# First attention of a two-layer graph-attention block: tiles 0 and 1 of a group as one task, tiles 2 and 3 one by one

## The chip, the core and the metric

The kernel runs on one core of one Trainium2 chip. The metric is the time of one execution in device microseconds (us). The kernel before has 6 runs, between 2294.36 and 2296.16 us, with a median of 2295.54 us. One execution was profiled.

## The reference

The input x has 128 batches of 64 nodes with 512 features. One 64 x 64 adjacency matrix holds for all batches. Everything is float32.

```python
def gat(x, adj, W, a):                      # [B,N,F] -> [B,H,N,O], all heads
    Wh = einsum('bnf,hfo->bhno', x, W)
    f1, f2 = Wh @ a[:, :O], Wh @ a[:, O:]
    e = f1[:, :, :, None] + f2[:, :, None, :]
    e = where(e > 0, e, 0.01 * e)
    e = where(adj > 0, e, -1e9)
    return einsum('bhnm,bhmo->bhno', softmax(e), Wh)

h = relu(layernorm(x))                      # 128 x 64 x 512
h = elu(gat(h, adj, W_heads, a_heads))      # 4 heads of 512, put side by side
out = elu(gat(h, adj, W_out, a_out))        # one head of 512
y = relu(out @ w1 + b1) @ w2 + b2 + out
return x + layernorm(y) * gamma + beta
```

## The kernel before

**Tiles and groups.** The 8192 rows (128 batches of 64) are 64 tiles of 128 rows: two batches in a tile. Four tiles make a group, and there are 16 groups (G = 4, NG = 16, lines 64 and 65). The large products (the first projection, the second projection, the two products of the feed-forward part) are done per group by a Winograd-like scheme with seven sub-products in place of eight (`unit`, line 242); a sub-product is a run of matmuls of 128 x 128 weights on 256 columns.

**First attention before the first projection.** From group 1 on, the attention weights of the first layer are applied to the normalized rows *before* the projection: per tile, `attend1` (lines 526 to 563) multiplies HN (the normalized rows, 128 x 512, line 345) with AT (the transposed attention weights, line 488) and writes the blocks z11, z12, zS1 and z22, which the first projection (`project1`, line 588) reads one group later. A tile holds two batches, rows 0 to 63 and rows 64 to 127, and each batch has its own matmul: the matmuls at line 547 contract over 64 rows, with b = 0 on the upper half of TensorE's rows and b = 1 on the lower half, and each b has a PSUM bank of its own. A tile has two halves of its features ("11" and "12" for tiles 0 and 1, "S1" and "22" for tiles 2 and 3). In the code a half is four matmuls; in the profile each float32 matmul has two records, so a half is 8 records and a tile 16. Half 0 writes two auxiliary PSUM banks (`aux`, line 93: 2 banks), half 1 writes two banks of the ring (`bank`, line 80: 6 banks). Each bank is then copied to z: b = 0 by ScalarE (line 559), b = 1 by VectorE (line 561). All other matmuls around this place use all 128 rows of TensorE.

**Where the tasks stand.** The main loop (line 948) goes over the groups. For a group g from 1 on it runs `project1(g)`, the first projection, whose last head's end stands just ahead of what concerns us: the ELU of its results (lines 571 to 573, on ScalarE and VectorE) still reads ring banks. Then comes `project2(g)` (line 677), 28 steps, each four matmuls in the code and eight records in the profile. Beside these steps `run` (line 233) spreads other work evenly: `first`, a list of 14 entries (lines 972 to 975), stands first in it, and holds the four attention tasks of the next group, the four transposes of the group before (`transpose_out`, line 777: four 128 x 128 transposes on TensorE, a copy on ScalarE at line 783, an addition on GpSimd at line 784), the normalization of two pairs of tiles of the group after next, and entries that do nothing. Their order in the groups 1 to 13 is: attention 0, transpose 0, nothing, attention 1, transpose 1, norms, nothing, attention 2, transpose 2, nothing, norms, attention 3, transpose 3, nothing. In group 14 there are no norms. Group 0 takes its attention tasks out of a table written by hand (lines 977 to 997).

**What sets the order.** Each engine executes its instructions in the order in which the program was built, and waits at semaphores. The weights of each sub-product come by DMA on the SyncE queue (SP in the profile) into a ring of 11 buffers (`piece`, line 211, tile w); a load waits until TensorE is done with the buffer that it takes. On GpSimd (POOL), `project2` also subtracts blocks of H1 head by head as TensorE finishes with each (line 688). The banks of the ring are given out in turn among those that are free first; each task thus waits for the last reader of the bank that it gets.

Of the kernel before, what the change touches and what calls it, by code (L numbers as in the profile page):

```python
# [9 lines left out]
FP = mybir.dt.float32  # L10
# [12 lines left out]
def gat_preln_kernel(  # L23
# [30 lines left out]
    nc = tc.nc  # L54
    P = 128
    B, N, F = x.shape
    H = W_heads.shape[0]
# [3 lines left out]
    NB = P // N  # L61
    KC = F // P
    NT = B * N // P
    G = 4
    NG = NT // G
    Q = O // 2
    T = 2 * P
# [6 lines left out]
    big = ctx.enter_context(tc.tile_pool(name="big", bufs=1))  # L74
# [5 lines left out]
    def bank(name):  # L80
        return ps.tile([P, 2, T], FP, tag="mm", name=name)
# [11 lines left out]
    def aux(shape, name):  # L93
        return ps.tile(shape, FP, tag="aux", name=name, bufs=2)
# [7 lines left out]
    X, HN, HNS, AT = {}, {}, {}, {}  # L102
# [126 lines left out]
    def flush_late():  # L229
        while late:  # L230
            late.pop(0)()

    def run(steps, side=()):

        side, done = list(side), 0
        for i, fn in enumerate(steps):
            fn()
            while done * len(steps) < (i + 1) * len(side):
                side[done]()
                done += 1  # L240
# [229 lines left out]
    def attn_weights(p):  # L470
        A1[p] = softmax(E1.pop(p), None, 2 * H, "s1", p)
# [23 lines left out]
    def stage_a(g):  # L495


        if g >= NG:
            return [], [], []
        p, r = 2 * g, 2 * g + 1  # L500

        def norms(p):
            norm1(2 * p)
            norm1(2 * p + 1)
            if p >= 2:
                ahead = 2 * p + (4 if p < 4 else 2)
                prefetch(ahead)
                prefetch(ahead + 1)

        def transposes(p):  # L510
            transpose_h(2 * p)
            transpose_h(2 * p + 1)

        return (
            [lambda: norms(p), lambda: norms(r)],
            [
                lambda: transposes(p), lambda: transposes(r), nothing, lambda: project_f(g), nothing,
                lambda: (scores1(g), attn_weights(p)), nothing, lambda: attn_weights(r),
            ],
            [nothing, lambda: transpose_weights(p), nothing, nothing, lambda: transpose_weights(r)],  # L520
        )
# [1 line left out]

    ZB = {}

    def attend1(g):
        z = {}
        ZB[g] = z

        def task(j):  # L530

            t = G * g + j
            at = AT[t]
            done = []
            for half in range(2):
                nm = ("11", "12")[half] if j < 2 else ("S1", "22")[half]
                if nm not in z:
                    z[nm] = big.tile([P, H, 2, T], FP, tag="z" + nm, name=f"z{nm}_{g}")
                src, off = (HNS[t], 0) if nm == "S1" else (HN[t], half * T)
                if half == 1:  # L540
                    banks = [bank(f"pz{nm}_{t}_{b}") for b in range(NB)]
                else:
                    banks = [aux([P, 2, T], f"pz{nm}_{t}_{b}") for b in range(NB)]
                for c in range(2):
                    for b in range(NB):
                        rows = slice(b * N, (b + 1) * N)
                        nc.tensor.matmul(
                            banks[b][:, c, :].rearrange("p (h n) -> p h n", h=H),
                            src[rows, off + c * P:off + (c + 1) * P],
                            at[rows, b], start=True, stop=True, skip_group_check=True,  # L550
                        )
                done.append((nm, banks))
            for nm, banks in done:
                for b in range(NB):
                    n0 = (j % 2) * P + b * N
                    dst = z[nm][:, :, :, n0:n0 + N].rearrange("p h c n -> p c h n")
                    srcv = banks[b].rearrange("p c (h n) -> p c h n", h=H)
                    if b == 0:
                        nc.scalar.copy(dst, srcv)
                    else:  # L560
                        nc.vector.tensor_copy(dst, srcv)

        return [lambda j=j: task(j) for j in range(G)]


    H1, ZSUM = {}, {}
# [11 lines left out]
    def z_sums(g, h):  # L578
        z = ZB[g]
        ZSUM[h] = new_sums(f"z{g}_{h}")  # L580
        sums(nc.gpsimd, z["S1"][:, h], z["11"][:, h], z["12"][:, h], z["22"][:, h], *ZSUM[h])
# [124 lines left out]
    def scores2(g, j):  # L706
        if j == 0:
            F2[g] = sm.tile([P, 2, G], FP, tag="f2", name=f"f2_{g}")
        f = F2[g]
        for c in range(2):  # L710
            junk = wk.tile([P, FO], FP, tag="elu", name=f"jf{g}_{j}_{c}", bufs=3)
            nc.vector.scalar_tensor_tensor(  # L712
                junk, WH2[g][:, j], 1.0, ao[:, c, :], ALU.mult, ALU.mult,
                accum_out=f[:, c, j:j + 1],
            )
# [45 lines left out]
    def stage_e(g):  # L761

        gap = [lambda: None]
        score = [lambda j=j: scores2(g, j) for j in range(G)]
        attend = [lambda q=q: attend2(g, q) for q in range(2)]
        return (
            gap + score + [lambda: spread2(g)] + gap * 2 + [lambda: softmax2(g)] + gap * 5
            + [lambda: transpose_weights2(g)] + gap * 2 + attend[0:1] + gap * 2 + attend[1:2] + gap * 4
        )
# [79 lines left out]
    def mix(*lists):  # L849

        lists = [l for l in lists if l]
        keyed = [((i + 0.5) / len(l), n, fn) for n, l in enumerate(lists) for i, fn in enumerate(l)]
        return [fn for _, _, fn in sorted(keyed, key=lambda k: k[:2])]
# [16 lines left out]
    norms, scores, turns = stage_a(1)  # L870
# [77 lines left out]
    for g in range(NG):  # L948
        if g >= 1:
            side = stage_e(g - 1)  # L950
            done, n = 0, 6 * H
            for i in range(n):
                if i % 6 == 0:
                    steps = project1(g, i // 6)
                steps[i % 6]()
                while done * n < (i + 1) * len(side):
                    side[done]()
                    done += 1
            flush_late()
        attn = attend1(g + 1) if g + 1 < NG else []  # L960
        norms, scores, turns = stage_a(g + 2)
        tr, ff, fin = feed_forward(g - 1) if g >= 1 else ([], [], [])
        if g == NG - 1:
            run(project2(g), tr + [nothing] * 6 + ff[:2])
            run(ff[2:], [
                lambda: [scores2(g, j) for j in range(G)], lambda: spread2(g), nothing, nothing,
                lambda: softmax2(g), *[nothing] * 7, lambda: transpose_weights2(g), nothing,
                *[lambda q=q: attend2(g, q) for q in range(2)], nothing,
            ])
            continue  # L970
        early = [lambda: z_sums(g + 1, 0)] if g else []
        first = mix(attn, tr, [nothing] * len(attn))
        if g >= 1:
            first[5:5] = norms[:1]
            first[10:10] = norms[1:]
        if g == 0:
            side = {
                0: lambda: (attend0(2, 1), turn0(1, 1), project_f(1)),
                1: lambda: (attend0(3, 1), turn0(2, 1)),
                2: lambda: (turn0(3, 1), scores1(1), attn_weights(2), attn_weights(3)),  # L980
                5: lambda: weight_sums(M1, LAST["pe"]),
                7: turns1[1],
                8: lambda: fetch(M2, LAST["pe"]),
                9: attn[0],
                10: lambda: (attn[1](), norms[0](), turns1[4]()),
                12: attn[2],
                13: lambda: (attn[3](), norms[1]()),
                15: scores[0],
                16: scores[1],
                17: lambda: weight_sums(M2, LAST["pe"]),  # L990
                18: scores[3],
                20: scores[5],
                21: scores[7],
                22: lambda: z_sums(g + 1, 0),
                26: turns[1],
                27: lambda: (turns[4](), load_rows()),
            }
            for i, fn in enumerate(project2(g)):
                fn()
                side.get(i, nothing)()  # L1000
        else:
            run(project2(g), first + mix(
                ff[:7] + early + ff[7:12] + fin[:1] + ff[12:13] + fin[1:2] + ff[13:],
                scores + [nothing] * 8,
            ) + mix(fin[2:], [nothing] + turns + [nothing] * 2))
    last = fin
    tr, ff, fin = feed_forward(NG - 1)
# [30 lines left out]
```

## Time and profile before

| | |
|---|---|
| median of 6 runs | 2295.54 us |
| the profiled execution, its own time | 2296.16 us |
| its span, first to last instruction | 2294.2 us |
| around the span (2296.16 - 2294.2) | 1.96 us |
| TensorE matmuls (PE) busy | 2274.1 us |
| TensorE weight loads (PEld) busy | 1890.6 us |
| VectorE (DVE), ScalarE (ACT), GpSimd (POOL) busy | 1274.0, 905.2, 1018.3 us |
| from one group's first attention task to the next group's | 140.37 us |

Busy time of PE counts each matmul from its start to its modelled end, and these overlap; so a busy PE may still lose time between matmuls. What counts is when one matmul starts after another. In the answers of the trace a row of the timeline is a run of like instructions: start in us from the span's start, duration of the run in us, engine, line, operation, what it writes and reads, the shape, and how many; in brackets stands the idle time of the engine ahead of it and what ended it.

### The profile page before, as it was taken

What the parts mean: (1) busy time and instruction counts of PE and PEld (TensorE: products, weight loads), DVE (VectorE), ACT (ScalarE), POOL (GpSimd) and SP (SyncE); (2) the same over time, 40 slices, a digit from 0 to 9 for tenths busy, and PEclk for the clock granted to TensorE, in tenths of its full rate; (3) what the DMA queues carried; (4) which work ended last, traced back from release to release, by engine and by line L of the source; (5) the groups of instructions that cost most, each with busy time, mean ns of one, the idle gap of its engine ahead of it and who ended that gap; (6) DMA issues with size and microseconds to landing.
All of it is one profiled execution on the core that took longest, in us unless ns stands there. A gap on an engine that the chain in (4) does not pass through costs nothing. (4 is left out here: it accounts for less than half of the span.)

```text
span 2294.2 us, 33256 instructions
## 1 busy us (share of the span) xinstructions
PE 2274.1 (99%) x11856; PEld 1890.6 (82%) x11856; DVE 1274.0 (56%) x2227; ACT 905.2 (39%) x1633; POOL 1018.3 (44%) x906
## 2 busy tenths in 40 slices
PE   9999999999999999999999999999999999999997
PEld 4688888888888888888888888888888888888885
DVE  7554654655556555564655646555475554744427
ACT  3535244252542525335253352534425244251512
POOL 7653524444254442634425344352444525533324
PEclk9999999999999999999999999999999999999999
DMA  8553453534535444353544545345354454635543
GB/s 289 194 183 130 147 179 133 180 132 147 175 132 185 136 156 160 135 184 131 166 150 140 182 133 179 130 147 179 133 180 133 147 174 132 183 118 171 160 147 106
DMA packets 255012, 361.15 MB, mean 157 GB/s; under 512 B 23768, under 2 KB 143608, under 8 KB 254848
## 3 DMA queue, kind: packets, MB, share of 16 engines
q1 hardware_dynamic: 250096, 341.93, 46.0%
q0 software_dynamic: 4576, 16.81, 2.0%
q8 instruction: 96, 1.57, 0.3%
q14 instruction: 68, 0.56, 0.1%
q10 hardware_dynamic: 176, 0.28, 0.0%
HBM read 331.66 MB, written 27.26 MB: 156 GB/s over the span
## 5 line engine op out<-in xcount | busy, mean ns | idle before, releaser
L305 PE MATMUL g_b<-w,h 128*128 128x256 f32 x2560 | 593.1, 379 | 0.0
L305 PEld LDWEIGHTS g_b<-w,h 128*128 128x128 f32 x2560 | 481.1, 190 | 64.6 <-issue 2.0
L289 PE MATMUL g_a<-z,w 128*128 128x256 f32 x1440 | 341.7, 380 | 0.0
L289 PE MATMUL g_a<-zs_z,w 128*128 128x256 f32 x1440 | 336.0, 381 | 0.0
L289 PEld LDWEIGHTS g_a<-zs_z,w 128*128 128x128 f32 x1440 | 269.9, 190 | 59.2 <-issue 24.3
L289 PEld LDWEIGHTS g_a<-z,w 128*128 128x128 f32 x1440 | 272.3, 190 | 41.3 <-DVE g_a L603 5.0
L305 PE MATMUL g_b<-w,hS 128*128 128x256 f32 x1024 | 238.2, 379 | 0.0
L607 POOL TENSOR_TENSOR hS<-hS,h 128x512 f32<-128x512 f32 x60 | 78.1, 1302 | 359.9 <-DVE hS L573 359.9
L305 PEld LDWEIGHTS g_b<-w,hS 128*128 128x128 f32 x1024 | 192.1, 190 | 25.0 <-issue 0.2
L571 ACT ACTIVATE exc<-g_a 128x512 f32<-128x512 f32 x240 | 142.6, 594 | 164.1 <-DVE g_a L603 96.2
L573 DVE SCALAR_TENSOR_TENSOR h<-exc,g_a 128x512 f32<-128x512 f32 x180 | 123.4, 686 | 140.9 <-ACT exc L572 140.3
L572 ACT ACTIVATE exc<-exc 128x512 f32<-128x512 f32 x240 | 151.4, 631 | 6.7
L688 POOL TENSOR_TENSOR h<-h,h 128x512 f32<-128x512 f32 x64 | 86.9, 1367 | 138.5 <-PE g_b L305 138.5
L688 POOL TENSOR_TENSOR h<-hS,h 128x512 f32<-128x512 f32 x64 | 81.7, 1277 | 146.2 <-PE g_b L305 146.0
L314 POOL TENSOR_TENSOR zs_z<-zS,z 128x512 f32<-128x512 f32 x60 | 85.3, 1422 | 137.2 <-PE g_a L289 134.0
L489 ACT COPY at<-s1pt 128x512 f32<-128x512 f32 x64 | 34.4, 590 | 268.9 <-PE s1pt L485 268.9
L833 POOL TENSOR_TENSOR xr<-xr,bs 128x512 f32<-128x512 f32 x64 | 96.4, 1510 | 74.3 <-DMA xr<-in_x_dram 44.4
L305 PE MATMUL g_d<-w,rt 128*128 128x256 f32 x512 | 121.8, 380 | 2.3 <-DVE o L825 1.0
L289 PE MATMUL g_c<-ot,w 128*128 128x256 f32 x512 | 122.7, 383 | 0.6 <-DVE ot L792 0.6
L289 PE MATMUL g_a<-zS,w 128*128 128x256 f32 x480 | 113.4, 379 | 0.0
L712 DVE SCALAR_TENSOR_TENSOR jf<-wh,ao 128x512 f32<-128x512 f32 x128 | 98.1, 802 | 26.6 <-ACT wh L694 26.4
L305 PEld LDWEIGHTS g_d<-w,rt 128*128 128x128 f32 x512 | 96.9, 190 | 17.4 <-DVE o L825 2.2
(164 smaller groups left out, 3531.0 us busy)
## 6 DMA issues: line engine op xcount, KB each, us to landing
w<-tc SPq DMA_DIRECT2D x624, 256.0 KB, 2.6
w<-in_L_gnn_W_out_dram SPq DMA_DIRECT2D x192, 256.0 KB, 2.7
w<-in_L_gnn_W_heads_dram SPq DMA_DIRECT2D x180, 256.0 KB, 2.9
w<-in_L_gnn_w_dram SPq DMA_DIRECT2D x96, 256.0 KB, 2.7
x<-in_x_dram SPq DMA_DIRECT2D x64, 256.0 KB, 4.6
xr<-in_x_dram SPq DMA_DIRECT2D x128, 128.0 KB, 2.6
out_dram<-o SPq DMA_DIRECT2D x126, 128.0 KB, 2.4
tc<-pt POOLq DMA_DIRECT2D x20, 512.0 KB, 4.3
```

Of the source, the lines that this page charges most:

```text
L289: LAST["pe"] = nc.tensor.matmul(bk[:, o, :], w[:, k, ts(o, P)], a[:, k, :], start=start and o == 0 and k == 0, stop=k == 1, skip_group_che ...
L305: LAST["pe"] = nc.tensor.matmul(bk[:, j, :], a[:, k, ts(j, P)], w[:, k, :], start=start and n == 0, stop=i == len(ms) - 1 and k == 1, skip ...
L314: eng.tensor_tensor(s2, s1, a11, ALU.subtract)
L489: nc.scalar.copy(AT[t].rearrange("p b h n -> p (b h) n"), pt)
L571: nc.scalar.activation(ex, src, AF.Relu, scale=-1.0)
L572: nc.scalar.activation(ex, ex, AF.Exp, scale=-1.0)
L573: nc.vector.scalar_tensor_tensor(dst, ex, -1.0, src, ALU.add, ALU.max)
L607: nc.gpsimd.tensor_tensor(dst, dst, H1["22"][:, h], ALU.add)
L688: nc.gpsimd.tensor_tensor(dst[:, h], x0[:, h], x1[:, h], ALU.subtract)
L712: nc.vector.scalar_tensor_tensor(junk, WH2[g][:, j], 1.0, ao[:, c, :], ALU.mult, ALU.mult, accum_out=f[:, c, j:j + 1],)
L833: nc.gpsimd.tensor_tensor(xr, xr, bs, ALU.add)
```

## The change

`attend1` gets a second argument, `paired`. Where it is true (in the loop's groups 1 to 14), tiles 0 and 1 are one task of four halves: tile 0 half 0 in the two auxiliary banks, tile 0 half 1 and tile 1 half 0 in two ring banks each, tile 1 half 1 in the two auxiliary banks again. Tiles 2 and 3 stay tasks of their own with the banks as before. The two copies of a half are now written directly behind its matmuls. The list `first` is written out so that the pair stands where attention 0 stood, and an entry that does nothing where attention 1 stood. In group 0 every tile stays a task of its own.

```diff
-    def attend1(g):
+    def attend1(g, paired):
         z = {}
         ZB[g] = z
-        def task(j):
+        def products(j, half, own):
             t = G * g + j
             at = AT[t]
-            done = []
-            for half in range(2):
-                nm = ("11", "12")[half] if j < 2 else ("S1", "22")[half]
...
-                if half == 1:
-                    banks = [bank(f"pz{nm}_{t}_{b}") for b in range(NB)]
+            nm = ("11", "12")[half] if j < 2 else ("S1", "22")[half]
...
+            if own:
+                banks = [aux([P, 2, T], f"pz{nm}_{t}_{b}") for b in range(NB)]
+            else:
+                banks = [bank(f"pz{nm}_{t}_{b}") for b in range(NB)]
+            for c in range(2):
+                for b in range(NB):
+                    rows = slice(b * N, (b + 1) * N)
+                    nc.tensor.matmul(
+                        banks[b][:, c, :].rearrange("p (h n) -> p h n", h=H),
+                        src[rows, off + c * P:off + (c + 1) * P],
+                        at[rows, b], start=True, stop=True, skip_group_check=True,
+                    )
+            for b in range(NB):
+                n0 = (j % 2) * P + b * N
+                dst = z[nm][:, :, :, n0:n0 + N].rearrange("p h c n -> p c h n")
+                srcv = banks[b].rearrange("p c (h n) -> p c h n", h=H)
+                if b == 0:
+                    nc.scalar.copy(dst, srcv)
                 else:
-                    banks = [aux([P, 2, T], f"pz{nm}_{t}_{b}") for b in range(NB)]
...
-        return [lambda j=j: task(j) for j in range(G)]
+                    nc.vector.tensor_copy(dst, srcv)
+        def task(js):
+            steps = [(j, half) for j in js for half in range(2)]
+            for i, (j, half) in enumerate(steps):
+                products(j, half, i == 0 or len(steps) == 4 and i == 3)
+        tiles = [(0, 1), (2,), (3,)] if paired else [(j,) for j in range(G)]
+        return [lambda js=js: task(js) for js in tiles]
...
-        attn = attend1(g + 1) if g + 1 < NG else []
+        attn = attend1(g + 1, g > 0) if g + 1 < NG else []
...
-        first = mix(attn, tr, [nothing] * len(attn))
+        gap = [nothing]
         if g >= 1:
-            first[5:5] = norms[:1]
-            first[10:10] = norms[1:]
+            first = attn[:1] + tr[:1] + gap * 2 + tr[1:2] + norms[:1] + gap
+            first += attn[1:2] + tr[2:3] + gap + norms[1:] + attn[2:] + tr[3:] + gap
```

## The prediction

> **What bounds the kernel.** I read the page first: span, busy time, granted clock. Then the waits of PE, the records of line 547, and last the timeline of PE, ACT and DVE around the four tasks of one group.
>
> ```profile
> span 2294.2 us, 33256 instructions
> PE 2274.1 (99%) x11856; PEld 1890.6 (82%) x11856; DVE 1274.0 (56%) x2227; ACT 905.2 (39%) x1633; POOL 1018.3 (44%) x906
> PEclk9999999999999999999999999999999999999999
> ```
>
> TensorE is busy 99% of the span, in every slice but the last, at full clock (0.998). The page's chain reaches back to 2263 us only, so it says nothing of the middle. The waits of PE say more: the longest in the whole trace are these, at the kernel's start and end.
>
> ```profile
> PE pab L177 <- DMA ar<-in_L_gnn_a_heads_dram: 4.8, 1, 4.8
> PE g_c L289 <- ACT t_c L255: 1.1, 1, 1.1
> ```
>
> So in the middle PE waits for nobody, and only work of TensorE, or time lost between its matmuls, can be saved. Line 547's own view shows such a loss: 58 of its 60 runs of weight loads begin after an idle time of PEld ended by "issue", that is by no other engine.
>
> ```profile
> L547 PE MATMUL pz<-at,hn x720: 376/376/480, 114.2 to 2059.5; 64*128 64x256 f32 x180
>   issue: 19.2, 58
> ```
>
> The PE timeline of the group that starts at 355.35 us tells the price:
>
> ```profile
> 355.35 2.00 PE L547 MATMUL pz<-at,hn 64*128 64x256 f32 x16
> 357.28 0.66 PE L782 MATMUL pto<-ident,o 128*128 128x128 f32 x4
> 357.77 1.89 PE L305 MATMUL g_b<-w,h 128*128 128x256 f32 x8
> 359.60 2.00 PE L547 MATMUL pz<-at,hn 64*128 64x256 f32 x16
> 361.53 0.66 PE L782 MATMUL pto<-ident,o 128*128 128x128 f32 x4
> 362.02 3.62 PE L305 MATMUL g_b<-w,h 128*128 128x256 f32 x16
> ...
> 373.96 1.89 PE L305 MATMUL g_b<-w,hS 128*128 128x256 f32 x8
> 375.69 0.59 PE L289 MATMUL g_c<-ot,w 128*128 128x256 f32 x2
> ```
>
> The last two rows give the undisturbed pace: 8 matmuls of 256 columns take 375.69 - 373.96 = 1.73 us from start to start, 0.216 each. The task at 359.60 is the second one (attention 1), which the change moves.
>
> **What one visit to the 64-row matmuls costs beyond its work.** (1) Before it: 8 full-row matmuls from 357.77 to 359.60 take 1.83 us, not 1.73: 0.10 lost. (2) The task: 16 records in 8 pairs, a pair side by side on the two halves of the rows. At 0.216 a pair this would be 1.73; from 359.60 to 361.53 it is 1.93: 0.20 lost. (3) Behind it, four transposes take 362.02 - 361.53 = 0.49. Without a visit ahead of them they take 0.44:
>
> ```profile
> 2178.15 0.60 PE L782 MATMUL pto<-ident,o 128*128 128x128 f32 x4
> 2178.59 1.89 PE L305 MATMUL g_b<-w,h 128*128 128x256 f32 x8
> ```
>
> so 0.05 is lost. The starts of the single records give the same without rounding: the first 64-row matmul comes 309 ns after the last full-row one (216 undisturbed: 93); the second pair 320 after the first (104); the first transpose 314 after the last pair (98); the second transpose 165 after the first (109 undisturbed: 56). The sum is 351 ns a visit, the same in every group within 3 ns.
>
> **The change, part by part.**
>
> *Removed.* One visit in each of the groups 1 to 14: the matmuls of attention 1 now follow those of attention 0, in the same row mode. That saves 14 x 0.351 = 4.91 us. The built order of the changed kernel agrees: on TensorE the 16 records stand ahead of transpose 0 in just these 14 groups, on ScalarE the copy of transpose 0 stands behind the two added copies, and on VectorE, GpSimd and SyncE the order is the same instruction by instruction. Group 0 has the same order on all engines.
>
> *Moved: transpose 1.* It now stands between full-row matmuls. The rows at 2178.15 show that such a transpose costs nothing beyond 0.44 us, work that it has today too. Cost 0.
>
> *Longer run.* No run in the trace is over 8 pairs. From pair 2 on, pairs come at 0.216 us like every 256-column matmul, in tiles of both kinds. I take 0 for pairs 9 to 16. Bounds: below 0.216 nothing goes, as 0.216 is the pace of all such matmuls here; at worst the start-up of 0.104 is paid once more in the middle, 14 x 0.104 = 1.46 us.
>
> *Added waits: banks.* Let S be the task's start (355.35). Halves 1 to 4 start at S, S + 0.97, S + 1.83 and S + 2.70 (4 pairs of 0.216 a half, and 0.104 once).
>
> ```profile
> 354.15 0.69 DVE L573 SCALAR_TENSOR_TENSOR h<-exc,g_a 128x512 f32<-128x512 f32 x1 [0.46 <-ACT exc L572]
> 355.89 0.69 DVE L573 SCALAR_TENSOR_TENSOR hS<-exc,g_a 128x512 f32<-128x512 f32 x1 [1.05 <-ACT exc L572]
> 356.63 0.69 DVE L561 COPY z<-pz 128x512 f32<-128x512 f32 x1
> ...
> 356.57 0.59 ACT L559 COPY z<-pz 128x512 f32<-128x512 f32 x1 [0.72 <-PE pz L547]
> ```
>
> Half 3 takes the ring banks of the last head's g5 and g1; their last reader is the L573 at 354.15, done at 354.84 = S - 0.51, and their first weight load stands at S + 1.62: 2.1 us to spare. Half 4 takes the auxiliary banks back. Half 1's copies end at 357.16 (ACT) and 357.32 (DVE) = S + 1.97; half 4's first weight load is due a slot ahead of its matmul, at S + 2.48: 0.5 us to spare, in each of the 14 groups (one group has ACT 0.28 us later, still in time). Transpose 0 takes the g6 bank, read until 356.58 and needed at S + 3.4. So I take 0 for the waits. Should the cover of half 4 go, each microsecond that the DVE copy is late beyond those 0.5 costs PE 1 us in each of 14 groups, with everything queued behind it on PE.
>
> *Copies.* Counts are unchanged: eight a pair. A half takes PE 0.864 us and its copies 0.59 on ACT and 0.69 on DVE side by side, so they keep up. ACT's copy of transpose 0 moves from 357.98 to about 359.8, transpose 1's keeps its place; both are read by g_c at 375.69. The additions of L784 on POOL follow.
>
> *Step delayed.* The second step of project2 (8 matmuls at 357.77) comes 1.73 us later. Its weight buffer is released that much later on SP's queue; the load into it is for a piece 11 further on, about 11 x 1.73 = 19 us away, and lands in 2.6 us. The subtraction at L688 that waits for this step (POOL, 359.81) moves to about 361.5, and is read in the p = 6 product after 380. All hidden; with the next step PE is 0.35 us ahead of before, as is every queue that waits for PE.
>
> What is late next? Nothing in the groups: PE has no other wait there, so the gain goes into the end unchanged.
>
> **Two rules of the Trainium skill.** PEld's idle time of 0.33 us ahead of each visit is the row. "TensorEngine Tiling (Array Packing)", Key Properties, says that a change of tiling mode drains TensorE, which agrees; "TensorE: Matmul & The Clock Gate", step-by-step, puts the drain at about 128 cycles, else hidden under the next matmul. By an estimate from that page (128 / 2.4 GHz = 53 ns, twice a visit) the gain would be 14 x 0.107 = 1.5 us, which no one could measure; the trace's 351 ns speak for 4.9. The first page's PSUM Bottleneck section speaks against the change: tiling speeds the matmuls, not the emptying of PSUM; here 0.69 against 0.864 us leaves that rule no hold.
>
> **The sum.** The profiled execution took 2296.16 us, 1.96 of it around the span: 2296.16 - 4.9 = 2291.3 with a span of 2289.3. The profiled run stands 0.62 above the median of the six, so for the median: 2295.54 - 4.9 = 2290.6 us, -0.21%. About 0.2%, 4.6 us, is what a measurement of this kernel can tell from no change, so the forecast lies close to that bound.
>
> **Rivals.**
> 1. *Start-up paid again* inside the 16 pairs, at the change of tile or at half 4's semaphore. For: no such run is in the trace. Against: at today's change of half pairs keep 0.216. Gain 4.91 - 1.46 = 3.45: 2292.1.
> 2. *Given back elsewhere*: some wait on PE, now hidden, takes the 0.35 us a group. For: SP's queue is in order and its loads do wait. Against: no wait on PE, and 19 us of lead. 2295.5. That the visits are not saved, though the order is as said, has the same price.
> 3. *Slower: auxiliary banks late.* Half 4 stalls on the DVE copy of half 1, which stands behind the ELU at L573. It decides when that copy ends after S + 2.48 + 0.35 = S + 2.83 (0.86 later than now). With two more DVE operations of 0.69 ahead of it: S + 3.35, 0.87 - 0.35 = 0.52 lost in 14 groups, 7.3 us: 2302.8. Against: DVE's order is unchanged.
>
> **How the numbers follow.** Forecast 0.84, rival 1 0.08, rival 2 0.05, rival 3 0.03. The six runs lie from 1.18 below to 0.62 above their median, so the forecast's median may miss the 0.2% bound, only 0.3 us away: I count 0.70 of its 0.84 beyond the bound and 0.14 within. Faster 0.70, same 0.14 + 0.08 + 0.05 = 0.27, slower 0.03. The range goes from 2290.6 - 1.2 = 2289.4 to rival 1 with a little scatter, 2292.3.
>
> **What would show it.** In line 547's view of after: 46 visits in place of 60, about 14.6 us of "issue" in place of 19.2 (14 x 0.33 less); one run of 32 records in about 3.73 us (2.00 + 8 x 0.216) ahead of transpose 0; tile 2's task 9.86 us behind S in place of 10.21; 140.02 us from group to group in place of 140.37; still no wait on PE. Wrong if the run of 32 takes over 3.8 us (rival 1 or 3, told apart by whether pair 13 waits for DVE), if the 140.02 fails while the run is right (rival 2), or if the transpose behind the delayed step starts late.

## The result, and the profile after

The changed kernel takes 2289.86 us (median of 19 runs, 2289.07 to 2291.24), the kernel before 2295.07 (39 runs beside them). The ratio is 0.9978, with a 95% interval from 0.9972 to 0.9984: 3.7 to 6.4 us faster. The forecast of 4.9 us lies inside, 2290.6 lies 0.7 above the median, and the range 2289.4 to 2292.3 holds it.

The page of after, its first lines:

```profile
span 2287.7 us, 33256 instructions
PE 2269.1 (99%) x11856; PEld 1892.9 (83%) x11856; DVE 1273.3 (56%) x2227; ACT 905.8 (40%) x1633; POOL 1016.2 (44%) x906
```

As many instructions as before, PE busy for 99% of the span as before. Neither line tells why the span is shorter. The view of the first attention's line (545 now, 547 before) does:

```profile
L545 PE MATMUL pz<-at,hn x720: 376/376/480, 112.9 to 2053.4; 64*128 64x256 f32 x180
...
  issue: 14.6, 44
```

The idle time of PEld ahead of these matmuls that no other engine ends fell from 19.2 us in 58 places to 14.6 in 44: the 14 visits that were forecast, at 0.33 us. The timeline of PE in the group shown before (it now begins at 353.74):

```profile
353.74 3.72 PE L545 MATMUL pz<-at,hn 64*128 64x256 f32 x32
357.39 0.66 PE L785 MATMUL pto<-ident,o 128*128 128x128 f32 x4
357.88 1.89 PE L305 MATMUL g_b<-w,h 128*128 128x256 f32 x8
359.61 0.60 PE L785 MATMUL pto<-ident,o 128*128 128x128 f32 x4
360.05 3.62 PE L305 MATMUL g_b<-w,h 128*128 128x256 f32 x16
363.60 1.14 PE L545 MATMUL pzS<-at,hns 64*128 64x256 f32 x8
```

The run of 32 records lasts 3.72 us (forecast 3.73). Transpose 1, between full-row matmuls, takes 360.05 - 359.61 = 0.44 us, and the 8 matmuls ahead of it 359.61 - 357.88 = 1.73: no loss on either side. Tile 2 follows at 363.60 - 353.74 = 9.86 us, as forecast. From one group's first attention matmul to the next group's, the records give 140.016 us in place of 140.367, twelve times within 3 ns: 0.351 a group.

The cover of half 4 held. In the timeline of the same group the copies of half 1 end at 355.55 (ACT) and 355.70 (DVE); half 4's weight load is due at 353.74 + 2.48 = 356.22:

```profile
354.27 0.69 DVE L576 SCALAR_TENSOR_TENSOR hS<-exc,g_a 128x512 f32<-128x512 f32 x1 [1.05 <-ACT exc L575]
354.96 0.59 ACT L555 COPY z<-pz 128x512 f32<-128x512 f32 x1 [0.72 <-PE pz L545]
355.01 0.69 DVE L557 COPY z<-pz 128x512 f32<-128x512 f32 x1
```

The two profiled executions differ by more, 6.5 us of span. Of these 1.4 lie ahead of the first matmul, which waits for its first DMA (4.8 us before, 3.4 after), and that time varies from run to run (3.8 to 4.3 us in the profiles of the runs below); 4.9 are the 14 groups; 0.2 are left.

### The profile page after: what moved, and what is told of

Its sections match the earlier page's. It is cut to its first block, busy times and chain, and to the rows that moved or that the text cites. A ratio compares the mean times of both kernels' runs of the same rounds, so it can differ in the third digit from the quotient of the medians.

```text
span 2287.7 us, 33256 instructions
## 1 busy us (share of the span) xinstructions
PE 2269.1 (99%) x11856; PEld 1892.9 (83%) x11856; DVE 1273.3 (56%) x2227; ACT 905.8 (40%) x1633; POOL 1016.2 (44%) x906
## 5 line engine op out<-in xcount | busy, mean ns | idle before, releaser
L691 POOL TENSOR_TENSOR h<-h,h 128x512 f32<-128x512 f32 x64 | 86.9, 1366 | 138.5 <-PE g_b L305 138.5
L314 POOL TENSOR_TENSOR zs_z<-zS,z 128x512 f32<-128x512 f32 x60 | 84.8, 1414 | 138.5 <-PE g_a L289 135.2
L691 POOL TENSOR_TENSOR h<-hS,h 128x512 f32<-128x512 f32 x64 | 81.7, 1277 | 138.9 <-PE g_b L305 138.7
L836 POOL TENSOR_TENSOR xr<-xr,bs 128x512 f32<-128x512 f32 x64 | 95.9, 1504 | 74.5 <-DMA xr<-in_x_dram 42.3
L715 DVE SCALAR_TENSOR_TENSOR jf<-wh,ao 128x512 f32<-128x512 f32 x128 | 94.7, 776 | 27.9 <-ACT wh L697 27.7
```

The costliest lines, as they stand in the source:

```text
L314: eng.tensor_tensor(s2, s1, a11, ALU.subtract)
L691: nc.gpsimd.tensor_tensor(dst[:, h], x0[:, h], x1[:, h], ALU.subtract)
L715: nc.vector.scalar_tensor_tensor(junk, WH2[g][:, j], 1.0, ao[:, c, :], ALU.mult, ALU.mult, accum_out=f[:, c, j:j + 1],)
L836: nc.gpsimd.tensor_tensor(xr, xr, bs, ALU.add)
```

## The experiments

All edits are to the changed kernel. "A group" is the distance between the first attention matmuls of two groups, in the profile, the twelve from group 1 to 13; visits are runs of line 545. Ratios are to the kernel before, timed beside each run. The changed kernel has 19 runs, e1, e2, e3 and e3b have 11 each, e4, e5, e6 and e8 five, e9 two.

| kernel | visits | a group, us | median, us | ratio, 95% interval |
|---|---|---|---|---|
| before | 60 | 140.367 | 2295.07 | 1 |
| changed | 46 | 140.016 | 2289.86 | 0.9978, 0.9972 to 0.9984 |
| e1, pair with the old banks | 46 | 140.303 | 2294.99 | 1.0001, 0.9992 to 1.0010 |
| e2, new banks, old places | 60 | 140.367 | 2295.99 | 1.0004, 0.9995 to 1.0013 |
| e3, two pairs | 32 | 140.566 | 2296.98 | 1.0008, 0.9999 to 1.0016 |
| e3b, two pairs, norms later | 32 | 139.713 | 2290.01 | 0.9975, 0.9966 to 0.9984 |
| e4, one visit | 18 | 139.437 | 2281.09 | 0.9940, 0.9927 to 0.9952 |
| e5, one visit, t3 early | 18 | 139.755 | 2286.66 | 0.9963, 0.9950 to 0.9977 |
| e8, one visit, norms early | 18 | 139.314 | 2280.66 | 0.9937, 0.9923 to 0.9950 |
| e6, halves apart | 88 | 141.506 | 2311.26 | 1.0068, 1.0056 to 1.0081 |
| e9, full rows | 46 | 145.870 | 2376.5 | 1.0352, 1.0322 to 1.0382 |

**Theory:** TensorE sets the time; each visit to the 64-row matmuls costs it 0.351 us beyond the work, and the ring banks only keep a longer visit from waiting. **Rivals:** the banks or the copies bring the gain; or the price belongs to something else in the task, such as its operands.

### The price: is it the row mode?

```diff
-                        src[rows, off + c * P:off + (c + 1) * P],
-                        at[rows, b], start=True, ...
+                        src[:, off + c * P:off + (c + 1) * P],
+                        at[:, b], start=True, ...
```

> The changed kernel with its first attention contracted over all 128 rows (the two batches of a tile are added up, so z is another quantity and the outputs are not the reference's; all other work is as it was). Copies, banks, places and waits stay. Each tile's 16 records now run one by one at 0.216 us in place of 8 pairs: 4 x 8 x 0.216 = 6.91 us a group more. Theory (the price of a visit is the change to 64-row matmuls and back): the three visits' 3 x 0.351 = 1.05 us go, 140.02 + 6.91 - 1.05 = 145.87 us a group, and no idle PEld ahead of line 545. Rival (the price comes from the new operands, banks or semaphores of the task): 146.92 us a group, with the idle times still there.

Measured: 145.870 us a group. Line 545 has no idle weight loads left. The timeline of PE:

```profile
364.74 7.07 PE L545 MATMUL pz<-at,hn 128*128 128x256 f32 x32
371.64 0.60 PE L785 MATMUL pto<-ident,o 128*128 128x128 f32 x4
```

32 records take 6.90 us to the transposes, 0.216 each, with nothing lost at either end: the first record of a visit comes 216 ns after the one before it (309 in the changed kernel), and the second transpose 109 ns after the first (165). Same tiles, banks, copies and semaphores: the 0.351 us belong to the change of row mode and back. (What e9 computes is another quantity; only its times are read.)

### The price: does it go by the visit?

e6 takes the pair apart into four visits, with the same banks:

```diff
+        if paired:
+            halves = [lambda i=i: products(i // 2, i % 2, i in (0, 3)) for i in range(4)]
+            return halves + [lambda: task((2,)), lambda: task((3,))]
...
+            first = attn[:1] + tr[:1] + attn[1:2] + gap + attn[2:3] + tr[1:2] + norms[:1] + attn[3:4] + gap
+            first += attn[4:5] + tr[2:3] + gap + norms[1:] + attn[5:] + tr[3:] + gap
```

> The four halves of tiles 0 and 1 as four visits, with work of project2 or a transpose between them, in the changed kernel's banks: 88 visits in place of 46. Theory (each visit has its price, whatever it holds): three more a group, each 0.093 + 0.104 + 0.098 + 0.104 = 0.40 us, as the new ones end in 256-column matmuls; 42 x 0.40 = 16.8 us above the changed kernel's 2289.9: 2306.7, 141.2 us a group. Rival (the price goes with the matmuls in the visit, or hides): under 2300.

Measured: 141.506 us a group, 2311.3 in all; above the forecast, and far from the rival. The timeline of PE around half 3:

```profile
361.00 1.13 PE L545 MATMUL pz<-at,hn 64*128 64x256 f32 x8
362.06 1.99 PE L305 MATMUL g_b<-w,h 128*128 128x256 f32 x8
363.89 0.60 PE L788 MATMUL pto<-ident,o 128*128 128x128 f32 x4
...
369.44 0.92 PE L545 MATMUL pzS<-at,hns 64*128 64x256 f32 x6 [0.23 <-ACT z L555]
```

A half is 4 pairs, 0.864 us; it takes 1.06: 0.20 lost. The 8 matmuls behind it take 1.83 in place of 1.73: 0.10. With 0.10 at the entry that makes the expected 0.40 a visit, 1.20 a group. The other 0.29 are a wait that the expectation missed: tile 2's first matmul waits for ACT's copy of half 4, since half 4, with the auxiliary banks, now stands just ahead of it, and that copy stands behind an hn on ACT. The matmul comes 608 ns after the one before it in place of 309; PE's own idle time shows 0.2 us of this (13 times, 2.9 us in all).

### The banks: e1 and e2

e1 keeps the pair and takes the banks in the old turn; e2 keeps the banks and puts the tiles back:

```diff
 e1
-                products(j, half, i == 0 or len(steps) == 4 and i == 3)
+                products(j, half, half == 0)
 e2
+                products(j, half, half == (paired and j == 1))
-        tiles = [(0, 1), (2,), (3,)] if paired else [(j,) for j in range(G)]
+        tiles = [(j,) for j in range(G)]
...
+            first = attn[:1] + tr[:1] + gap + attn[1:2] + tr[1:2] + norms[:1] + gap
+            first += attn[2:3] + tr[2:3] + gap + norms[1:] + attn[3:] + tr[3:] + gap
```

> Tiles 0 and 1 stand side by side in one task as in the changed kernel, but the banks alternate as before: half 3 (tile 1, half 0) takes the two auxiliary banks again. Theory (a saved visit is worth 0.351 us, and the four ring banks are what keeps PE from waiting): half 3's first weight load is due at S + 1.62 us, and half 1's copies end at S + 1.81 (ACT) and S + 1.97 (DVE); PE stalls 0.3 to 0.6 us in each of 14 groups, so the gain of 0.351 is eaten: 2294.4 to 2298.6 us against 2295.1 before, and a wait on PE or PEld for DVE z or ACT z appears 14 times. Rival (only the place of the task counts, banks are free anyway): 2290, as the changed kernel.

> Four tasks at their old places, so 60 visits as before; but tile 1 takes ring banks for its half 0 and auxiliary banks for its half 1, and the copies are written behind each half, as in the changed kernel. TensorE's order is that of the kernel before. Theory (only the saved visits count): no change, 2295.1 within 0.6 us, 140.37 us from group to group. Rival (the banks or the place of the copies bring the gain): 2290.

e1 measured 2295.0, the gain gone. Its timeline shows the wait:

```profile
354.34 4.01 PE L545 MATMUL pz<-at,hn 64*128 64x256 f32 x32
...
355.56 0.59 ACT L555 COPY z<-pz 128x512 f32<-128x512 f32 x1 [0.72 <-PE pz L545]
...
356.19 1.75 PEld L545 LDWEIGHTS pz<-at,hn 64*128 64x128 f32 x16 [0.26 <-ACT z L555]
```

The run lasts 4.01 us in place of 3.72. Half 3's weight load was due at 354.34 + 1.62 = 355.96 and begins at 356.19, just behind ACT's copy (355.56 + 0.59 = 356.15). That takes 0.29 of the 0.351 us, 14 times; of the 0.06 that are left, 0.9 us in all, its profile loses most again in one place of group 13 (told at the end). So the ring banks are what makes the pair pay; they are needed only because the pair is there. e2 shows the other half of this: with the new banks and copies at the old places a group takes 140.367, exactly as before. Its median is 1.0 us above that of the kernel before beside it, inside its interval but outside the 0.6 us of the expectation; in its profile the same place in group 13, where g_c waits for the sum at L795, loses 0.9 us more than in the kernel before.

### More tiles in a visit: e3, e3b, e4

```diff
 e3
+        tiles = [(0, 1), (2, 3)] if paired else [(j,) for j in range(G)]
+            first = attn[:1] + tr[:1] + gap * 2 + tr[1:2] + norms[:1] + gap
+            first += attn[1:2] + tr[2:3] + gap + norms[1:] + gap + tr[3:] + gap
 e3b: the tiles of e3
+            first = attn[:1] + tr[:1] + gap * 2 + tr[1:2] + gap * 2
+            first += attn[1:2] + norms[:1] + tr[2:3] + norms[1:] + gap + tr[3:] + gap
 e4
+                products(j, half, i % 3 == 0)
+        tiles = [(0, 1, 2, 3)] if paired else [(j,) for j in range(G)]
+            first = attn[:1] + tr[:1] + gap * 2 + tr[1:2] + norms[:1] + gap
+            first += gap + tr[2:3] + gap + norms[1:] + gap + tr[3:] + gap
```

> Tiles 2 and 3 become a second task of four halves at tile 2's place. Two visits a group, so by the saved visits alone 14 x 0.351 = 4.9 us below the changed kernel: 2285.0. But there ScalarE normalizes two tiles (hn, L346) and copies s_b ahead of the first zS copy: in the changed kernel that copy ends 3.4 us after the visit's start, and half 4's weight load on its bank is due at 2.48. If the banks' theory holds, half 4 stalls about 1 us in 14 groups: 0.65 to 0.8 us a group slower than the changed kernel, 2299 to 2301. Rival (the wait is hidden or the copies move ahead): 2285.

> Two pairs as in e3, but the first pair of norms stands behind the second pair of tiles, so that ScalarE has no hn ahead of the zS copies. Theory (e3 lost 1.0 us a group on its auxiliary bank, because of ScalarE's order): the wait on ACT zS goes, two visits a group are left, 140.37 - 2 x 0.351 = 139.66 us a group; the second visit ends in a 256-column matmul here and not in transposes, 0.05 us more: 139.71, and 2289.9 - 14 x 0.30 = 2285.7 in all. Rival (two pairs a group don't work, whatever ScalarE's order): at or above 2295, as e3.

> All four tiles of a group are one task of eight halves at tile 0's place (halves 1, 4 and 7 in the auxiliary banks, the others in ring banks). One visit a group in place of three: 2 x 14 x 0.351 = 9.8 us below the changed kernel, 2280.0 us, if a half's copies (0.59 on ACT, 0.69 on DVE) keep up with its 0.864 us on TensorE, as no other ACT work stands among them here. The run of 64 records should take about 2.00 + 24 x 0.216 = 7.18 us. Rival (PSUM emptying sets the pace of a long run, or the ring runs out): waits on PE for z copies and a time at or above the changed kernel's 2289.9.

e3, a visit fewer than the changed kernel, is 0.55 us a group slower. Its timeline in the second visit, which begins at 364.36:

```profile
366.51 0.81 ACT L346 ACTIVATE hn<-x,n1nb,n1rs 128x512 f32<-128x512 f32 x1
367.23 0.57 ACT L555 COPY zS<-pzS 128x512 f32<-128x512 f32 x1
...
367.85 0.73 PEld L545 LDWEIGHTS pz<-at,hn 64*128 64x128 f32 x8 [1.03 <-ACT zS L555]
```

DVE's copy of the same half began at 365.57. ACT's began 1.7 us later, as two hn (and a copy of s_b between them) stand ahead of it in its queue, and half 4 waited. PE lost 0.90 us a group and won 0.35; the place was as expected, the size of the wait a tenth too high, and the 2297.0 in all lie below the 2299 to 2301 that were expected. e3b only moves the norms behind the visit, and a group takes 139.713 us; the forecast was 139.71. So ScalarE's order was the whole loss. In all it took 2290.0 and not 2285.7: in the profile 4.2 us go in one place of group 13 (told at the end).

e4 won 13.9 us; the forecast was 2280.0. Its run of 64 records goes at 0.216 a pair to the end:

```profile
352.74 3.72 PE L545 MATMUL pz<-at,hn 64*128 64x256 f32 x32
...
359.85 0.66 PE L785 MATMUL pto<-ident,o 128*128 128x128 f32 x4
```

From its start to the transposes are 7.11 us, 32 pairs of 0.216 and the 0.20 of the visit, so PSUM's emptying does not set the pace. But 139.437 a group is 0.12 above the 139.31 that three visits fewer should give. The timeline some 20 us behind the visit:

```profile
372.46 1.69 ACT L346 ACTIVATE hn<-x,n1nb,n1rs 128x512 f32<-128x512 f32 x2 [2.96 <-POOL n1nb L344]
...
374.06 0.56 ACT L786 COPY ot<-pto 128x512 f32<-128x512 f32 x1
...
374.65 1.66 DVE L795 TENSOR_TENSOR ot<-ot 128x512 f32<-128x512 f32 x1 [4.56 <-ACT ot L786]
...
376.36 1.99 PE L289 MATMUL g_c<-ot,w 128*128 128x256 f32 x8
```

Two hn, then the copy of transpose 3, then DVE's sum (until 376.31), then g_c, each as soon as the one ahead of it ends. The 8 matmuls take 1.99, not 1.89: 0.10 of a new start-up. Two kernels, with the tiles and banks of e4, each change the order of the list to test this:

```diff
 e5: transposes 2 and 3 ahead of the norms
+            first += tr[2:3] + gap + tr[3:] + norms[1:] + gap * 3
 e8: the norms ahead of transpose 2
+            first += norms[1:] + tr[2:3] + gap * 3 + tr[3:] + gap
```

> The one visit of eight halves as in e4, with transposes 2 and 3 moved ahead of the second pair of norms. e4 took 139.43 us a group where three saved visits give 140.37 - 3 x 0.351 = 139.31; its trace shows TensorE's g_c matmuls late by 0.11 us a group, behind the sum at L795 on VectorE, which waits for ScalarE's copy of transpose 3, which stands behind two hn of 0.81 us each. Theory (that queue is the rest): 139.31 us a group, 14 x 0.113 = 1.6 us below e4's 2281.1: 2279.5. Rival (a long run of 64-row matmuls has a cost of its own): 139.43 as e4, 2281.1.

> The one visit of e4, with the second pair of norms one entry ahead of transpose 2 in place of moving transpose 3: its statistics wait for a matmul 1.7 us earlier, so both hn should leave ScalarE before transpose 3's copy is due, and VectorE's order around the sums is not changed as in e5. Theory (e4's rest of 0.11 us a group is ScalarE's queue, nothing of the long visit): 139.31 us a group, 2279.5. Rival 1 (the long visit itself costs it): 139.43 and 2281.1. Rival 2 (the chain of statistics, GpSimd and hn collides elsewhere again, as in e5): a new wait on PE, 139.5 or more.

e5: the wait at g_c is gone, and a larger one stands elsewhere; 139.755 us a group is neither the forecast nor the rival. The waits of PE, and the timeline:

```profile
PE pth L362 <- ACT hT L364: 3.4, 13, 1.4
```

```profile
373.34 0.20 DVE L332 TENSOR_SCALAR n1ve<-n1mv 128x1 f32<-128x1 f32 x2
...
374.51 1.71 POOL L691 TENSOR_TENSOR hS<-h,h 128x512 f32<-128x512 f32 x1
376.18 1.52 POOL L334 TENSOR_TENSOR n1rs<-n1ve,mhalf 128x1 f32<-128x1 f32 x2
...
377.99 1.52 ACT L346 ACTIVATE hn<-x,n1nb,n1rs 128x512 f32<-128x512 f32 x2 [7.14 <-POOL n1nb L344]
```

The sums at L795 and L314, ready earlier, now stand on DVE between the statistics of the norms and their end, which comes at 373.54 (370.09 in e4). But that is not what hn waited for: GpSimd, which works without a break from 368.7, has transpose 3's addition (L787) and one more subtraction (L691) ahead of the norms' step at L334, and reaches it at 376.18, 2.6 us after DVE is done (371.51 in e4). So hn leaves ACT at 379.5 in place of 374.1, and the copies of the h transposes behind it are late: 0.44 us a group on PE. e8 moves the statistics instead; hn starts at 370.87, g_c goes without a break, no wait on PE is left in the groups, and a group takes 139.314 us, the forecast 139.31: rival 1, a price of the long visit itself, falls. Its median, 2280.66, is 1.2 us above the forecast and not told apart from e4's by their intervals; by the profile it is 0.12 us a group better.

## Why the prediction was right, point by point

- *Bound.* TensorE's stream sets the time; right. In the kernels that were run every difference a group is accounted for by visits, by e9's longer work and by waits on PE that the trace names.
- *Price of a visit, 0.351 us, and 14 visits fewer.* Right: 140.367 - 140.016. e9 shows that the row mode is what costs, e6 that it goes by the visit.
- *The rule of the Trainium skill.* "TensorEngine Tiling (Array Packing)", Key Properties, says that a change of mode drains TensorE; e9 shows that the change costs time, and no run shows whether a drain is what costs. The prediction's estimate of 1.5 us, from a drain of 128 cycles, was too small by a factor of 3.3: 0.351 us a visit against 0.107.
- *Longer run at no cost.* Right, up to 64 records (e4, e8); rival 1 falls.
- *Cover of half 4.* Right: no wait. e1 (at half 3) and e3 show the price when a bank comes late: 0.29 us a group where a copy is late by 0.2, 0.90 where ScalarE's queue makes it late by 1.0. Rival 3 named VectorE as the engine that would be late; where it happened it was ScalarE.
- *The delayed step of project2, and "what is late next: nothing".* Right at 0.35 us a group, and rival 2 falls. It is not right without limit: at 1.05 us (e4) the next wait was ScalarE's queue.
- *The sum.* 4.9 forecast, 5.2 measured, with an interval of 3.7 to 6.4. The runs don't show the 0.3 to be more than scatter.

## What to carry to other kernels

Where TensorE never waits, compare starts of neighbouring matmuls: what comes later than its pace, with idle weight loads ended by no engine, may be the price of a change of tile shape, which here is paid per visit. The idle weight loads alone don't tell (the full-row loads at L629 of the kernel before show 27.7 us of them); the same kernel with full rows does. Put such work together until the copies out of PSUM, in the order in which they stand on their engines, can't return the banks in time; for each bank taken again, count back from its weight load to the last copy and look at what is queued ahead of that copy. When one wait is removed by moving a step, look at what the moved step now stands in front of.

## What was not expected of the hardware

After a pause TensorE came back slowly, in one profile. In e3b's group 13, two additions at L836 stand ahead of the norms' step (L334) on GpSimd, hn comes late, and g_c waits 2.3 us for the sum at L795. The timeline of PE, and the windows around it (the granted clock is the number ahead of the last two):

```profile
1917.26 3.57 PE L289 MATMUL g_c<-ot,w 128*128 128x256 f32 x8 [2.33 <-DVE ot L795]
```

```profile
1917.00:1922.00 5.00, 4.74 (x15) 3.93 (x16) 4.61 (x4) 1.60 (x4) 5.00 (x4) 0.66 0.74 234
1922.00:1936.00 14.00, 14.00 (x97) 12.05 (x96) 2.50 (x4) 4.45 (x10) 4.30 (x4) 1.00 0.42 132
```

The first distance between the matmuls behind the pause is 0.589 us and the next six are 0.427, about twice 0.216, while the clock granted is 0.66 in this window (0.50 from 1917.06 to 1920.47), and 1.00 in the next. So a wait of 2.3 us cost 4.2 in all. Pauses of 0.6 us (e3), 0.8 us (e2) and 1.4 us (e5) had no such echo. e3b's runs spread over 3.8 us, those of the changed kernel over 2.2; whether each of them lost as much is not known. "TensorE: Matmul & The Clock Gate" of the Trainium skill, Part 1, tells of a clock halved after an idle window of about 3.4 us; here 2.3 us of idle time were enough.

This place in group 13, where the norms are the last ones and two of GpSimd's additions at L836 (L833 before) stand ahead of their step, makes group 13 longer than the groups ahead of it by 0.17 us in the kernel before, 0.24 in the changed one, 0.35 in e3, 0.92 in e1 and 1.05 in e2, beside the 4.2 in e3b. In e1 and e2 the second of these additions waits 0.90 and 0.84 us for its DMA (xr), in the kernel before and the changed one not at all, which is about the difference. No run moved these additions, so what sets the length in the other kernels is open.
